# SyncE's queue in a twelve-layer macaron network: the program's order instead of the scheduler's

## The chip, the cores and the metric

The kernel runs on one NeuronCore of a Trainium2 chip. The metric is the device time of one execution in microseconds (us), as the median over runs; lower is better. Times inside the kernel come from one profiled execution.

## What is computed

The input x has 4 x 1024 tokens of 128 features in float32. Twelve residual layers follow each other: three groups of "half a feed-forward, attention, half a feed-forward" whose feed-forwards differ by level, and a fourth of the same shape with ternary weights. Each layer reads a layer norm of x and adds its result to x:

```python
x = x + 0.5 * L0_ffn(norm(x)); x = x + L0_attn(norm(x)); x = x + 0.5 * L0_ffn(norm(x))
x = x + 0.5 * L1_ffn(norm(x)); x = x + L1_attn(norm(x)); x = x + 0.5 * L1_ffn(norm(x))
x = x + 0.5 * L2_ffn(norm(x)); x = x + L2_attn(norm(x)); x = x + 0.5 * L2_ffn(norm(x))
x = x + 0.5 * L3_ffn(norm(x)); x = x + L3_attn(norm(x)); x = x + 0.5 * L3_ffn(norm(x))
```

L0's and L1's attentions are softmax attentions with 16 heads of 8 features (L0's is causal and has more behind it); L2's and L3's are linear attentions. L0_ffn works on values rounded to four-bit floats. What the change bears on most are the mixtures L1_ffn and L2_ffn, where each token goes to two of eight experts. L2's, shortened:

```python
shared = silu(x @ shared_w1.T) @ shared_w2.T
top_k_gates, top_k_idx = top_k(x @ gate_w.T, 2)
gates = zeros((T, 8)); gates[arange(T)[:, None], top_k_idx] = softmax(top_k_gates, axis=1)
h = einsum('td,ehd->teh', x, experts_w1)
expert_out = einsum('teh,edh->ted', silu(h), experts_w2)
out = shared + einsum('ted,te->td', expert_out, gates)
```

L1's expert has two up projections, `silu(g) * u`, and there is no shared part.

## The kernel before

x stays in the on-chip memory SBUF in eight tiles of 512 tokens. The program is written as generators that are advanced in turns: a main line (attention, or one half of a mixture), and beside it side lines such as the routing of the next layer or the return of rows of the last. Behind the written program a scheduler places the instructions: it keeps the data dependencies, and gives each engine (TensorE or PE, VectorE or DVE, ScalarE or ACT, GpSimd or POOL, SyncE or SP) an order of its own planning, which can differ from the order in which the program emits them. An engine then works through its queue strictly in that order; an instruction that waits holds up those behind it.

SyncE computes nothing. It issues nearly all plain transfers and reads registers: the loads of x and of weights (`load` L306, `load_x` L313), the queries and keys of a softmax attention in `laid_out` (L565), the row maxima in `maxima` (L609, L610), everything that a mixture fetches and stores, and the final output (L1232). Gathers and scatters by index are issued by GpSimd.

**A mixture.** There are four mixture layers, numbers 3, 5, 6 and 8 of the twelve layers counted from 0; 3 and 5 are L1's and 6 and 8 L2's. Each is done in two halves of 2048 tokens; "8.1" is the second half of layer 8. The front of a half routes its tokens and scatters their normed rows, sorted by expert, into a buffer `rows_in` in HBM (L1348, GpSimd). The half then runs over 23 tiles of 256 rows, each with one expert's weights. `fetch` gets tile j:

```python
w = pool.tile([P, WIDE], F32, tag="w", name="w", bufs=3)
first = nc.sync.value_load(half.which[:, j : j + 1], min_val=0, max_val=(E - 1) * P)
nc.sync.dma_start(out=w[:, :width], in_=self.weights[bass.ds(first, P), :])
xr = pool.tile([P, RT, D], F32, tag="xr", name="xr", bufs=3)
got = nc.sync.dma_start(out=xr..., in_=k.rows_in[half.h][j * TT : (j + 1) * TT, :]...)
```

That is a register read of the expert's row (L1399), the weights w (L1400; 768 KB in L1, 512 KB in L2) and the rows xr (L1402; 128 KB). w and xr have three buffers each, so a load waits until the tile three before has released its buffer. w is released by the last down matmul (L1447), xr by its transposes (L368, tr<-ident,xr).

`tiles` works on tile j: `turned` transposes the rows on TensorE, and ScalarE copies them to xT (L1420); the up matmuls (L1464) read w and xT; ScalarE and VectorE form h; the down matmuls (L1447) of the tile before follow; `leave` scales the result (yo), transposes it, copies it to yr (L1432, two buffers), and SyncE stores it to `rows_out` (L1433). In the written program, after the first group of up matmuls of tile j:

```python
if c + many == NC:
    ahead = turned(half.fetched[0][1]) if half.fetched else None
yield from downs()
waiting = [(j, w, c + i, h[:, i, :]) for i in range(many)]
if c == 0:
    if j + 2 < NTT:
        self.fetch(half, j + 2)
```

So a fetch is written two tiles ahead of its use, behind the down matmuls of tile j-1, and the transposes of the next tile's rows stand ahead of down matmuls. At the end of a half the first tiles of the next half are fetched, as far as its routing is known. After the last tile, `back` gathers the rows to the tokens (L1515, GpSimd) and VectorE adds them to x (L1502).

**Softmax attention.** Heads are done in groups of four, for a batch of 1024 tokens. For a coming group, `laid_out` brings queries and keys into a buffer `qk` by four transfers (L565); for the running one, `maxima` computes scores (L587), reduces them (L597), and sends the row maxima through memory into a further row of `qk` (L609, L610); the second pass of scores (L747) reads them.

The load of the L3 feed-forward's weights, `l3f_w` (2816 KB), is written where that layer begins, between the halves of layer 8.

Of the kernel before, what the change touches and what calls it, by code (L numbers as in the profile page):

```python
# [1525 lines left out]
def program(arrays):  # L1526
    nc = bacc.Bacc("TRN2", target_bir_lowering=False, num_devices=1)
    ins = {
        k: nc.dram_tensor(f"in_{k}", v.shape, mybir.dt.from_np(v.dtype), kind="ExternalInput").ap()
        for k, v in arrays.items()  # L1530
    }
    out = nc.dram_tensor("out", (B * S, D), F32, kind="ExternalOutput").ap()
    with tile.TileContext(nc) as tc, ExitStack() as ctx:
        _Kernel(ctx, tc, ins, out).run()
    return nc

# [6 lines left out]
```

## Time and profile before

| | |
|---|---|
| median of three runs | 4999.24 us (4991.68 to 5002.0) |
| the profiled execution | 5007.68 us, span 5005.9 us |
| mean granted TensorE clock | 0.909 |
| PE, DVE, ACT, POOL busy | 4282.1, 2664.7, 1707.0, 958.7 us |
| first L0 feed-forward | 0 to 230 us |
| L0 attention | 230 to 1240 us |
| second L0 feed-forward, front of layer 3 | 1240 to 1550 us |
| layer 3 (L1 mixture) | 1550 to 1950 us |
| L1 attention | 1950 to 3100 us |
| layer 5 (L1 mixture) | 3100 to 3450 us |
| layer 6 (L2 mixture), L2 attention begun | 3450 to 3880 us |
| L2 attention, layer 8 (L2 mixture) | 3880 to 4280 us |
| L3 | 4280 to 5006 us |

The profile shows each engine's instructions with start and duration in us. A row of the timeline is: start, duration, engine, line, operation, output<-inputs, shapes, count, and in brackets the idle time just before with what ended it. "SPq" is SyncE's queue: the time that an issue takes there, not that of the transfer. A row of waits is: engine and instruction <- what it waited for: us in total, times, longest. The granted clock is TensorE's, as a share of its full speed. In the timeline four up matmuls of a tile last 1.03 us at the full clock.

### The profile page before, as it was taken

The numbers are of one execution on the slowest core, as the hardware profiler recorded it, in microseconds if no ns is written. First come the engines' busy times: TensorE is split into PE (matmuls) and PEld (weight loads), VectorE is DVE, ScalarE is ACT, GpSimd is POOL, SyncE is SP. The second block draws the span as 40 slices with busy tenths as digits, with TensorE's granted clock in tenths as the row PEclk, the third lists the DMA queues.
The fourth block names the chain that finished last, engine by engine and source line by source line (L and its number), as shares of the span: only waits on it lengthen the run. The fifth ranks groups of instructions, "written<-read, shape, count | busy, mean of one in ns | idle before, by whom it ended". The sixth has DMA issues, their size and how long they took to land.

```text
span 5005.9 us, 62914 instructions
## 1 busy us (share of the span) xinstructions
PE 4282.1 (86%) x23628; PEld 2223.6 (44%) x23628; DVE 2664.7 (53%) x5900; ACT 1707.0 (34%) x3077; POOL 958.7 (19%) x1296
## 2 busy tenths in 40 slices
PE   4799999999757787999999998887877677899999
PEld 3533333333446654333333335765555456344444
DVE  8656757573875353666767673344555544221310
ACT  1134444444222112554545454222222222243322
POOL 4312222221253212001010101213232322200000
PEclk8799999997878897999989999998988798999999
DMA  2000000000002432000010001533332234000000
GB/s 86 5 5 9 3 9 3 9 4 6 1 33 87 152 122 69 6 6 12 8 35 6 12 4 62 170 122 115 113 108 88 74 122 155 20 1 0 0 9 9
DMA packets 112282, 232.51 MB, mean 46 GB/s; under 512 B 20519, under 2 KB 77351, under 8 KB 110315
## 3 DMA queue, kind: packets, MB, share of 16 engines
q1 hardware_dynamic: 95595, 194.91, 12.5%
q0 software_dynamic: 16384, 33.59, 2.3%
q8 instruction: 187, 3.06, 0.3%
q14 instruction: 116, 0.95, 0.1%
HBM read 170.47 MB, written 49.56 MB: 44 GB/s over the span
## 4 chain that ended last, share of the span: by engine, by line
PE 68%; DVE 13%; issue 5%; POOL 5%; another core or an unknown queue 5%; ACT 2%; DMA 1%; SPq 0%; POOLq 0%; DVEq 0%; ACTq 0%
PE sc L747 17%; PE acc L677 9%; PE big L1209 9%; PE big L1464 8%; PE acc L1447 5%; PE big L587 4%; PE tr L368 4%; PE big L1193 1%; POOL ln_rs L355 1%; POOL y L1515 1%; DVE xn L358 1%; PE big L1374 1%; DVE part L597 1%; PE acc L1380 1%
## 5 line engine op out<-in xcount | busy, mean ns | idle before, releaser
L752 ACT ACTIVATE es<-sc 128x512 f32<-128x512 f32 (+3 forms) x1792 | 893.6, 549 | 979.7 <-PE sc L747 566.5
L597 DVE TENSOR_REDUCE part<-big 128x2 f32<-128x1024 f32 (+3 forms) x768 | 886.1, 1158 | 444.7 <-PE big L587 334.6
L747 PE MATMUL sc<-qk 32*128 32x512 f32 (+3 forms) x3584 | 1068.7, 617 | 37.0 <-ACT es L752 29.4
L587 PE MATMUL big<-qk 32*128 32x512 f32 (+3 forms) x3584 | 967.9, 621 | 37.0 <-DVE part L597 17.3
L1464 PE MATMUL big<-xT,w 128*128 128x256 f32 x2208 | 571.9, 398 | 101.3 <-ACT xT L1420 57.3
L747 PEld LDWEIGHTS sc<-qk 32*128 32x128 f32 x3584 | 354.1, 190 | 445.7 <-issue 273.8
L677 PE MATMUL acc<-es,va 128*32 128x256 f32 (+2 forms) x6144 | 528.0, 416 | 1.6 <-POOL es L755 1.4
L1464 PEld LDWEIGHTS big<-xT,w 128*128 128x128 f32 x2208 | 428.9, 200 | 192.6 <-ACT xT L1420 64.4
L1209 PE MATMUL big<-h,l3f_w 128*128 128x512 f32 x1024 | 449.3, 596 | 15.9 <-ACT h L1216 12.6
L355 POOL TENSOR_TENSOR ln_rs<-ln_ve,neg_half 128x4 f32<-128x4 f32 x120 | 124.8, 1041 | 1631.8 <-DVE ln_ve L354 1608.6
L1447 PE MATMUL acc<-h,w 128*128 128x256 f32 x1472 | 393.1, 399 | 37.3 <-DVE h L1361 31.7
L1348 POOL DMA_INDIRECT rows_in<-xn,rows x256 | 249.0, 973 | 571.0 <-DVE rows L1023 163.9
L1515 POOL DMA_INDIRECT y<-rows_out,rows x256 | 244.7, 956 | 542.0 <-DMA xr<-rows_in 242.3
L677 PEld LDWEIGHTS acc<-es,va 128*32 128x32 f32 x6144 | 124.6, 110 | 498.4 <-issue 442.4
L587 PEld LDWEIGHTS big<-qk 32*128 32x128 f32 x3584 | 283.6, 191 | 86.5 <-DVE part L597 38.4
L1447 PEld LDWEIGHTS acc<-h,w 128*128 128x128 f32 x1472 | 279.3, 202 | 86.6 <-DVE h L1361 34.4
L755 POOL TENSOR_SCALAR_AFFINE_SELECT es<-es 128x128 f32<-128x128 f32 x512 | 174.6, 350 | 704.2 <-ACT es L752 698.5
L1209 PEld LDWEIGHTS big<-h,l3f_w 128*128 128x128 f32 x1024 | 192.7, 191 | 252.2 <-issue 231.1
L1472 ACT ACTIVATE h<-big 128x512 f32<-128x512 f32 x184 | 109.7, 597 | 507.7 <-PE big L1464 375.9
L1360 ACT ACTIVATE h<-big 128x1024 f32<-128x1024 f32 x124 | 126.7, 1024 | 431.4 <-PE big L1464 190.9
L1473 DVE TENSOR_TENSOR h<-h,big 128x512 f32<-128x512 f32 x184 | 126.1, 686 | 195.0 <-ACT h L1472 168.9
L358 DVE TENSOR_SCALAR xn<-x,ln_mv,ln_rs 128x128 f32<-128x128 f32 x352 | 108.5, 358 | 194.8 <-POOL ln_rs L355 89.1
(279 smaller groups left out, 4786.6 us busy)
## 6 DMA issues: line engine op xcount, KB each, us to landing
w<-in_l1f_w SPq DMA_DIRECT2D x92, 768.0 KB
w<-in_l2f_w SPq DMA_DIRECT2D x92, 512.0 KB
xr<-rows_in SPq DMA_DIRECT2D x184, 128.0 KB
rows_out<-yr SPq DMA_DIRECT2D x184, 128.0 KB
qk<-qd SPq DMA_DIRECT2D x128, 64.0 KB
rows_in<-zero SPq DMA_DIRECT2D x4, 1472.0 KB
rows_in<-xn,rows POOLq DMA_INDIRECT x256
y<-rows_out,rows POOLq DMA_INDIRECT x256
```

Source lines behind the costliest of these rows:

```text
L355: nc.gpsimd.tensor_tensor(rs, ve, self.neg_half, ALU.pow)
L368: self.nc.tensor.transpose(ps[:n, i * P : (i + 1) * P], t, self.ident)
L587: nc.tensor.matmul(ps[:, j, :w], lhsT=qk[rows, 0, bass.ts(q, P)], rhs=qk[rows, 1, c : c + w], start=True, stop=not diag,)
L597: nc.vector.tensor_reduce(to[:, 2 * pair : 2 * pair + 2, t], ps[:, :, :w], AX.X, ALU.max, negate=True)
L677: nc.tensor.matmul(out[0][32 * i : 32 * i + 32, lo:hi], lhsT=self.vas[b % 2][:, kc, (4 * g + i) * (HD + 1) :][:, :32], rhs=es[i][:, lo:hi] ...
L747: nc.tensor.matmul(ps[:, off:], lhsT=qk[rows, 1, bass.ts(kc, P)], rhs=qk[rows, 0, qb * BLK + off : (qb + 1) * BLK], start=True, stop=True,)
L752: nc.scalar.activation(es[i][:, off:], ps[:, off:], AF.Exp, scale=ISQ)
L1209: nc.tensor.matmul(ps[:, j, :], lhsT=m[:, i * FF + (2 * pair + j) * P : i * FF + (2 * pair + j + 1) * P], rhs=hs[z][:, i, :], start=i == 0 ...
L1348: put = nc.gpsimd.indirect_dma_start(out=k.rows_in[half.h][:, :], out_offset=bass.IndirectOffsetOnAxis(ap=at, axis=0), in_=xns[t // TPB][: ...
L1447: nc.tensor.matmul(outs[j][:, :TT], lhsT=w[:, low + c * D :][:, :D], rhs=h, start=c == 0, stop=c == NC - 1)
L1464: nc.tensor.matmul(ps[:, i, :], lhsT=w[:, bass.ts(col, P)], rhs=xT, start=True, stop=True)
L1515: nc.gpsimd.indirect_dma_start(out=y, out_offset=None, in_=k.rows_out[half.h][:, :], in_offset=bass.IndirectOffsetOnAxis(ap=self.rows[:, i ...
```

## The change

All of SyncE's instructions, transfers and register reads, are put into its queue in the order in which the program emits them. The other engines stay with the scheduler. No transfer is added or removed, and no buffer changes.

```diff
     out = nc.dram_tensor("out", (B * S, D), F32, kind="ExternalOutput").ap()
     with tile.TileContext(nc) as tc, ExitStack() as ctx:
+        ctx.enter_context(tc.manual_schedule(engines={mybir.EngineType.SP}))
         _Kernel(ctx, tc, ins, out).run()
     return nc
```

In SyncE's queue, the steady part of a mixture's half changes as follows (T register read, W weights, x rows, o store of result rows; the number is the tile, here of half 8.1):

```text
before  x14 W12 o9   x15 W13 o10   x16 W14 o11   (T read in batches, far ahead)
after   T12 W12 x12 o9   T13 W13 x13 o10   T14 W14 x14 o11
```

At the beginning of a half, before had W0, W1, W2 ahead, with the rows between them and behind; after has T0 W0 x0, T1 W1 x1, T2 W2 x2. The load of `l3f_w` moves from behind W12 of half 8.0 to the place between the two halves. In the softmax attentions, the four query and key transfers of a coming group stand as a block behind the maxima rows of the group before, where they stood between them.

## The prediction

> **What bounds the kernel now.** I read the page first (engines, then the chain that ended last), then the windows by stage, SyncE's waits, and the timeline of single tiles in the stages where SyncE works.
>
> ```profile
> PE 4282.1 (86%) x23628; PEld 2223.6 (44%) x23628; DVE 2664.7 (53%) x5900; ACT 1707.0 (34%) x3077; POOL 958.7 (19%) x1296
> ...
> PE 68%; DVE 13%; issue 5%; POOL 5%; another core or an unknown queue 5%; ACT 2%; DMA 1%; SPq 0%; POOLq 0%; DVEq 0%; ACTq 0%
> ```
>
> TensorE is busy for 86% of the span and carries 68% of the chain. Data transfers carry 1% and SyncE's queue 0%: today almost nothing waits for what SyncE issues. So little can be won by another order on SyncE, and what it can lose depends on how near its loads stand to their use. That differs by stage:
>
> ```profile
> 1550.00:1950.00 400.00, 334.02 (x1517) 255.12 (x1517) 173.95 (x430) 83.40 (x160) 81.94 (x85) 0.91 0.40 129
> 1950.00:3100.00 1150.00, 1095.03 (x8380) 387.33 (x8381) 733.11 (x1119) 585.22 (x1072) 75.72 (x80) 0.94 0.06 14
> 3450.00:3880.00 430.00, 316.33 (x1360) 230.61 (x1358) 226.32 (x707) 102.72 (x159) 133.80 (x140) 0.87 0.33 102
> 3880.00:4280.00 400.00, 286.36 (x1276) 212.71 (x1276) 205.64 (x588) 97.17 (x154) 118.49 (x123) 0.87 0.35 112
> ```
>
> (Stretch, its length, busy time of PE, PEld, DVE, ACT, POOL, granted clock, DMA share, GB/s.) Attention leaves TensorE 55 us of 1150 and moves 14 GB/s. The mixtures of L1 (first row) and L2 (last two rows) move 102 to 129 GB/s, and there SyncE fetches, tile by tile, the weights (w) and the rows (xr).
>
> ```profile
> 4213.03 1.03 PE L1464 MATMUL big<-xT,w 128*128 128x256 f32 x4
> 4213.23 0.34 SPq L1400 DMA_DIRECT2D w<-in_l2f_w  x1
> 4215.10 0.38 PE L368 MATMUL tr<-ident,xr 128*128 128x128 f32 x2
> 4215.31 1.89 PE L1447 MATMUL acc<-h,w 128*128 128x256 f32 x8
> 4215.51 0.32 SPq L1402 DMA_DIRECT2D xr<-rows_in  x1
> 4217.04 1.03 PE L1464 MATMUL big<-xT,w 128*128 128x256 f32 x4
> 4217.24 0.34 SPq L1400 DMA_DIRECT2D w<-in_l2f_w  x1
> ```
>
> This is the undisturbed tile of L2, 4.01 us from one w load to the next, with TensorE filled. The w issued at 4213.23 went out when the down matmuls of three tiles earlier released its buffer; its up matmuls follow at 4217.04, 3.81 us later. Between them, at 4215.10 (+1.87), TensorE transposes the rows of the very same tile, and only then come the down matmuls that release the next w buffer. The xr issued at 4215.51 isn't this tile's: it takes the buffer that the transposes have just released and serves a tile two further on. Rows are about two tiles ahead of weights in SyncE's queue.
>
> **The change part by part.** Compared by order, TensorE, VectorE, ScalarE and GpSimd keep their steady order; SyncE's alone changes, with the same transfers.
>
> *(1) Rows behind weights.* In program order a fetch issues the register read, then w(j+2), then xr(j+2), and then comes rows_out(j-1). So xr(j+2) leaves right behind w(j+2), which still waits for its buffer. The old trace has this sequence once, by chance, at the start of the last half:
>
> ```profile
> 4128.75 0.34 SPq L1400 DMA_DIRECT2D w<-in_l2f_w  x1
> 4129.14 0.43 SPq L1402 DMA_DIRECT2D xr<-rows_in  x1
> ```
>
> The packets of that xr end at 4132.33, 3.58 us after the w was issued, behind those of the w (4131.99). From last packet to use there is about another half microsecond: where the up matmuls did wait for w, its packets had ended 3.62 after its issue at 4241.28 and the matmul began 4.20 after it,
>
> ```profile
> 4245.48 1.10 PE L1464 MATMUL big<-xT,w 128*128 128x256 f32 x4 [0.23 <-DMA w<-in_l2f_w]
> ```
>
> So the transposes of tile j+2 can start about 3.58 + 0.5 = 4.1 us after w(j+2) was issued, not at +1.87: 2.2 us late. Behind them on TensorE stand the down matmuls (1.9 us) that release the next w, so the delay is inside the loop and comes back in each tile: 4.1 + 0.2 + 1.9 = 6.2 us instead of 4.0. DVE's and ACT's work for the tile, and the row stores, wait for TensorE in the same loop.
>
> Weighed against a rule: the Trainium skill, "DMA: Bandwidth & Descriptors", section "Anatomy of one DMA — SWDGE (gpsimd) path", fits one transfer at 2.0 us plus bytes over 436 GB/s (for GpSimd's path). An estimate from it for 128 KB, issued 0.39 behind w, is 0.39 + 2.3 = 2.7 us, a delay of 0.8 per tile. But it gives 3.2 us for the 512 KB of w, where the trace's use is at 4.2, and it knows no transfer ahead in the queue. I take the row, and keep the rule as a low end.
>
> How many tiles? For each of L2's 92 tiles I took from the timeline the time from the w issue to the transposes of its rows (tr); where that is under 4.1, the tile is late by the difference. Halves are named by the layer's number (0 to 11) and the half, in their order in time:
>
> - 6.0: 13 tiles, 27.4 us; 6.1: 14 tiles, 25.5 us; 8.0: 12 tiles, 22.1 us; 8.1: 20 tiles, 42.2 us. Raw sum 117 us.
>
> The other tiles have attention, routing or shared-expert matmuls between (tr at +4.2 to +13) and don't mind. Part of the sum falls ahead of stalls that have another end: TensorE idles 19.1 us in tile 4 of 6.0, 15.9 and 9.7 in tiles 4 and 5 of 6.1, 11.3 and 13.5 in tiles 2 and 15 of 8.0, 24.1 in tile 4 of 8.1, mostly in VectorE's queue behind gathers of rows (`DVE x L1502 <- DMA y<-rows_out,rows`, 111.1 us in the waits). Those gathers don't move when a tile ahead of them is late. Taking each stall of over 9 us as swallowing what is late before it, there remain 13.0 + 16.2 + 8.6 + 36.7 = 74.5 us; letting every idle of over 2 us swallow, 2.1 + 2.3 + 8.6 + 36.7 = 50 us. I take the middle, **+62 us**. With 3.6 instead of 4.1 (no half microsecond to use) the two are 53.5 and 36; with the rule's 2.7 they are 20 and 17.
>
> *(2) L1's 92 tiles: nothing.* Their tile takes 5.62 us and 768 KB of w; the release of a w buffer stands earlier, and tr comes 7.37 us after w in the undisturbed tile, 5.24 at the least. A w here lands in about 4.0, xr 0.4 to 0.6 behind it, with use at about 5: cover of over 2 us in the steady tile. If that were gone, it would cost up to 1 us for some 45 steady tiles.
>
> *(3) Starts of halves.* Before, three w's were issued ahead, whatever the rows waited for; now w1 and w2 stand behind xr0, which waits for the scatter of its rows. At 8.0 that wait ends at 3912.5; w1 goes out some 0.8 us later and is used at 3918.6 in the old trace, so 0 to +2 us, swallowed by the 11.3 us in tile 2. At 6.0, 6.1 w1 is about 4 us late, ahead of the stalls in tile 4. I put 0 net, bounds 0 and +10.
>
> *(4) The 2816 KB load of l3f_w.* Before, it is issued at 4025.92 in the middle of 8.0 and makes one w land at +7.0 (1.5 us of idle). Now it goes ahead of w0 of 8.1, some 8 us of packets, where tile 4's 24 us hide it. -1.5 to +3; I put 0.
>
> *(5) Register reads.* 23 in each half, 0.57 us each on SyncE. They were hoisted in batches; now one stands ahead of each w, while SyncE waits for the buffer anyway. 0; bare, 0.57 x 30 steady tiles = 17 us.
>
> *(6) Attention.* SyncE's largest waits are here:
>
> ```profile
> SPq L609 <- DVE mrows L607: 1020.4, 58, 55.7
> SPq L565 <- PE sc L747: 386.2, 15, 51.3
> ```
>
> The second is queries of a group two ahead that wait for a buffer, with the maxima rows of the running group behind them. In program order they come after that group's. But TensorE waits for such a transfer (`PE big L587 <- DMA qk<-qd`) only 4.5 us in all. 0, bounds -30 (a third of the 101 us that TensorE idles in both softmax stages) and +10.
>
> **Sum.** 62 + 0. The profiled execution took 5007.68 us (span 5005.9), so it would be 5070; it stands 8.4 above the median of three runs, 4999.24, on which I put the sum: **5061 us**.
>
> **The clock.** Holes of 2.2 us each 6.2 us could throttle TensorE. In the trace a hole of 1.94 us (tile at 1586.8) left the matmuls at 1.03 us for four, but
>
> ```profile
> 3721.85 1.67 PE L1464 MATMUL big<-xT,w 128*128 128x256 f32 x4 [1.96 <-issue]
> ```
>
> shows four matmuls at 1.67 after a hole of 1.96 with another of 1.12 before it. The Trainium skill, "TensorE: Matmul & The Clock Gate", section "HAM oscillation — how this bites in real kernels", tells of a loop with short compute and a wait for each tile that starts cold in every tile, for idle over about 3.4 us. By its limit our hole costs nothing; by the row some windows do. By the row at its worst, 0.6 us per four matmuls, a tile's 16 cost 2.6, times some 28 tiles that keep their delay: +73.
>
> **Rivals.**
>
> *Clock or queue on top (slower still).* The holes throttle, or the delays of (2) and (5) come bare: 62 + 50 gives about 5110, up to 5150. For it: the row above. Against: work stays at two thirds of the time.
>
> *Hidden.* xr lands as the rule says (+17 to +20) and stalls take the rest: 4999 to 5015. For it: half of L2's time already is stalls. Against: the last 18 tiles of 8.1 have none, and their lag is measured from rows.
>
> *Faster.* One mechanism: in attention, loads whose buffer is free no longer stand behind queries whose buffer isn't. Place: L565 ahead of the maxima rows in L1's and L0's attention; price up to -30, with L2's loss at its low 17: -13, 4986. It decides once attention gives back more than L2 loses, so over 50 us by my size, half of TensorE's idle there. Against it: the 4.5 us.
>
> *No effect.* The order would differ on paper only. Against: the order of SyncE's queue in the changed program does differ in each L2 tile.
>
> **How the numbers follow.** A measurement of this kernel can tell about 0.2%, 10 us, from no change. Likeliest case (5035 to 5100): 0.68. Slower still: 0.12. Hidden: 0.10, of which 0.03 ends over +10. Faster: 0.10. So slower 0.83, same 0.07, faster 0.10. Range: from 5000 (half of the hidden case) to 5130.
>
> **What would show it.** In the changed trace: w-to-w in the last half's tiles about 6.2 us; each xr 0.4 behind its w; TensorE's idle ended by xr at the transposes (L368); the stretch of 8.1 longer by some 35 us, L1's mixtures, both softmax attentions and L3 unchanged to within 5; granted clock near 1.0 in the tail. Wrong if the tile stays at 4.0 (xr not late), or if attention moves by over 10 us.

## The result: 2.9% slower, and the profile after

The changed kernel takes 5140.34 us (median of four runs, 5125.11 to 5153.8) against 4996.27: a ratio of 1.0287, 95% interval 1.0254 to 1.0320. The forecast was 5061 us with a range up to 5130. The direction was right, the size was not: +144 us where +62 was worked out. The profiled execution (5135.53 us, span 5133.5) is 128 us above that of before.

The page of the changed kernel, engines and chain:

```profile
PE 4346.9 (85%) x23628; PEld 2252.5 (44%) x23628; DVE 2674.7 (52%) x5900; ACT 1710.7 (33%) x3077; POOL 959.6 (19%) x1296
...
PE 67%; DVE 12%; issue 6%; POOL 6%; DMA 4%; another core or an unknown queue 2%; ACT 2%; SPq 0%; POOLq 0%; DVEq 0%; ACTq 0%
```

Transfers were 1% of the chain and are 4%. Which transfers, the waits of TensorE say for the two L2 mixtures and the linear attention between them (3450 to 4420 us; us in total, times, longest):

```profile
PE tr L368 <- DMA xr<-rows_in: 147.8, 56, 40.3
PE tr L368 <- DVE yo L1426: 38.8, 10, 11.3
PE acc L1447 <- DVE h L1361: 28.4, 4, 19.8
```

The first line is 3% of the span: transposes waiting for rows. In the kernel before, no wait of TensorE is put down to xr. Three of the 56 waits stand at starts of halves. 40.3 us at 8.0 are for the scatter, and TensorE idled there before too (48.9 us, with no releaser named); 8.2 us more are in 8.0 and 13.4 us at the first rows of 8.1. The other 53 add up to 85.8 us. The undisturbed tile, on TensorE and on SyncE (rows of other instructions left out):

```profile
4335.23 1.03 PE L1464 MATMUL big<-xT,w 128*128 128x256 f32 x4
4338.22 0.41 PE L368 MATMUL tr<-ident,xr 128*128 128x128 f32 x2 [1.97 <-DMA xr<-rows_in]
4338.46 1.89 PE L1447 MATMUL acc<-h,w 128*128 128x256 f32 x8
4340.19 1.03 PE L1464 MATMUL big<-xT,w 128*128 128x256 f32 x4
```

```profile
4334.34 0.35 SPq L1400 DMA_DIRECT2D w<-in_l2f_w  x1
4334.74 0.42 SPq L1402 DMA_DIRECT2D xr<-rows_in  x1
4335.88 0.32 SPq L1433 DMA_DIRECT2D rows_out<-yr  x1
4340.39 0.36 SPq L1400 DMA_DIRECT2D w<-in_l2f_w  x1
```

xr goes out 0.40 us behind its w; its transposes begin 3.88 us after the w; the down matmuls follow and release the next w at 4340.39. w to w is 6.05 us instead of 4.01 (the median of the last 17 tiles is 6.01).

By stage, from the first up matmuls of each half in both traces: at the first tile of layer 3 the changed kernel is 13.5 us behind (L0's attention), at layer 6 24.8 (L1's attention), at the last tile of 8.1 125.7. The two L2 mixtures, with the attention between them, thus cost 101 us and the two softmax attentions 29 (13.5 and 15.4); L1's mixtures give back 4, L3 adds 2.

### The profile page after: what moved, and what is told of

Same layout as the page of the kernel before. It is cut to its first block, busy times and chain, and to the rows that moved or that the text cites. A ratio compares the mean times of both kernels' runs of the same rounds, so it can differ in the third digit from the quotient of the medians.

```text
span 5133.5 us, 62740 instructions
## 1 busy us (share of the span) xinstructions
PE 4346.9 (85%) x23628; PEld 2252.5 (44%) x23628; DVE 2674.7 (52%) x5900; ACT 1710.7 (33%) x3077; POOL 959.6 (19%) x1296
## 4 chain that ended last, share of the span: by engine, by line
PE 67%; DVE 12%; issue 6%; POOL 6%; DMA 4%; another core or an unknown queue 2%; ACT 2%; SPq 0%; POOLq 0%; DVEq 0%; ACTq 0%
PE sc L747 17%; PE acc L677 9%; PE big L1209 8%; PE big L1464 6%; PE acc L1447 6%; PE big L587 5%; PE tr L368 4%; DMA xr<-rows_in 3%; POOL y L1515 2%; PE big L1193 1%; POOL rows_in L1348 1%; POOL ln_rs L355 1%; PE big L1374 1%; DVE part L597 1%
## 5 line engine op out<-in xcount | busy, mean ns | idle before, releaser
L1464 PE MATMUL big<-xT,w 128*128 128x256 f32 x2208 | 582.9, 403 | 50.0 <-issue 39.0
L1447 PE MATMUL acc<-h,w 128*128 128x256 f32 x1472 | 406.8, 410 | 32.6 <-DVE h L1361 28.4
```

What stands on the lines that cost most here:

```text
L1447: nc.tensor.matmul(outs[j][:, :TT], lhsT=w[:, low + c * D :][:, :D], rhs=h, start=c == 0, stop=c == NC - 1)
L1464: nc.tensor.matmul(ps[:, i, :], lhsT=w[:, bass.ts(col, P)], rhs=xT, start=True, stop=True)
```

## The experiments

Runs of one group share a chip, and each ratio is to the kernel before beside them. Its level differs from group to group: 4996 us beside the result, 4861 to 4867 in the first two groups and the last, and 5017 in the third. Differences of times are formed within a group. The diffs are shortened to the lines that matter, and their comments are added.

**First group: which part of the program.** The region is opened only for some turns of the main loop in `run`:

```diff
-            for _ in steps:
-                self.tick()
+            if mixture:                      # e_attention: if not mixture
+                with self.tc.manual_schedule(engines={mybir.EngineType.SP}):
+                    for _ in steps:
+                        self.tick()
+            else:
+                for _ in steps:
+                    self.tick()
```

Program order in the mixtures' turns alone:

> SyncE follows the program's order only while a mixture's half is the main line; in the attentions, L0 and L3 the scheduler places its instructions as before. Theory (rows late in L2): xr leaves behind its w as in the changed kernel, an undisturbed tile of L2 takes about 6.0 us instead of 4.0, and some 95 of the 128 us that the profiled executions differ by are here: about 5095 us; both softmax attentions as before. Rival (attention and the clock carry the loss, and L2's stalls absorb the late rows): under 5050. Rival (weights no longer fetched ahead at the starts of halves are what counts): here the scheduler may still place a w across the region's edge, so L2 would lose only some 30 us: about 5030.

4949.95 against 4862.29 us, 1.0176 (1.0159 to 1.0193): +88 us. Half 8.1's tile takes 6.06 us. The larger part of the loss is here, as the theory said. The kernel with the rest:

> The complement: SyncE follows the program's order only while the main line is no mixture (both softmax attentions, the L0 and L3 feed-forwards and linear attentions); in the mixtures the scheduler places it as before. Theory: the tiles of L2 take 4.0 us as before; L1's attention is 15 to 20 us longer, because the scheduler, which plans TensorE with SyncE's order given, groups eight maxima matmuls of a new group together at three of its four batches; with L0's attention +20 to +30 in all: about 5020 us. Rival (the difference in attention is chance of the clock from one execution to the next): 4996 within 10. Rival (attention carries most of the loss): over 5060.

4902.37 us, 1.0079 (1.0062 to 1.0096): +40 us, with the tile at 4.01. Neither rival holds, chance (within 10 us) or most of the loss (over 60 us), and the size is above the 20 to 30 us that were expected.

Then the rows. The changed kernel, with xr written ahead in `tiles`:

```diff
                 if c + many == NC:
                     ahead = turned(half.fetched[0][1]) if half.fetched else None
+                    while half.got < min(NTT, j + 5):
+                        half.ahead.append(self.rows_of(half))     # the xr transfer of fetch, moved here
                 yield from downs()
```

> The changed kernel (SyncE in program order everywhere), but the program itself asks for the rows earlier: xr of tile j+4 is written right behind the transposes that release its buffer, ahead of the down matmuls and of w of tile j+2. Theory: rows are in time, an undisturbed tile of L2 takes 4.0 us again, the 18 tiles at the end of half 8.1 give back 35 us and L2 in all 60 to 90; attention keeps its loss of about 30, the starts of halves 10 to 30: 5040 to 5060 us. Rival (weights' order or register reads slow the tile): the tile stays near 6.0 and the time near 5135.

4886.46 us, 1.0043 (1.0027 to 1.0060): +24 us, about half of what was expected, the tile at 4.01. And the same with program order in the mixtures' turns only:

> Both: SyncE in program order only while a mixture is the main line, and the rows written two tiles further ahead. Theory: the rows are in time and attention is the scheduler's: 4996 to 5020 us, what is left being the starts of halves. Rival: as for the run with program order in the mixtures alone, if rows are not the cause: about 5090.

4850.34 us, 0.9979 (0.9971 to 0.9988): 12 us faster than before. It differs from the first run of this group only in where the program writes xr, and by 100 us. Late rows carry L2's loss, and program order as such costs the mixtures nothing.

**Second group: behind what, and L1's attention.** The kernel before and the changed one, on this chip:

> The kernel before once more, unchanged, for a trace from the same chip as the runs beside it. Both theories: within 0.2% of its own runs, tile of L2 4.0 us.

> The changed kernel once more, unchanged, beside the others on one chip. Theory (a sum of its parts: late rows +100, attention +40): ratio 1.027 to 1.030, tile of L2 5.95 us. Rival (the loss depends on the chip, for instance on its throttling): ratio under 1.02.

Before: 4858.74 us in one run. Changed: 4972.31, 1.0214 (1.0197 to 1.0231), between theory and rival: the tile is 6.03 us, as on the first chip, and from the first tile of layer 6 to the last of 8.1 the traces part by another 96 us, as the 101 there. What is smaller here is the rest. The parts of the first group, 88 and 40, add up to 23 us more than the 105 us of the whole. The traces place most of that in attention: against the one trace of before at this level, L1's attention loses 27 us in the run with program order in the attentions and 9 us in the changed kernel, L0's 26 and 14. For L1 the reason is a wait of 12.7 us that only the whole change removes (shown under "Attention" below).

Next, two statements of `fetch` exchanged:

```diff
-        w = pool.tile(...)
-        first = nc.sync.value_load(...)
-        nc.sync.dma_start(out=w[:, :width], ...)
         xr = pool.tile(...)
         got = nc.sync.dma_start(out=xr..., ...)
+        w = pool.tile(...)
+        first = nc.sync.value_load(...)
+        nc.sync.dma_start(out=w[:, :width], ...)
```

> The changed kernel with two statements of fetch exchanged: the rows xr of tile j+2 are written ahead of the register read and of w of the same tile, so they leave SyncE before it waits for w's buffer, but only one tile earlier than in the changed kernel. Theory (what counts is standing behind a transfer that waits, not how far ahead the program asks): the tile is 4.0 us again, and the ratio that of the run with rows written further ahead, 1.002 to 1.008. Rival (rows must be two tiles ahead): tile over 5 us, ratio over 1.015.

4888.96 us, 1.0043 (1.0026 to 1.0060), the same as with rows written two tiles ahead. Its SyncE:

```profile
4079.78 0.32 SPq L1433 DMA_DIRECT2D rows_out<-yr  x1
4080.14 0.43 SPq L1399 DMA_DIRECT2D xr<-rows_in  x1
4082.57 0.35 SPq L1407 DMA_DIRECT2D w<-in_l2f_w  x1
```

xr leaves 2.43 us before w, while SyncE would otherwise stand waiting for w's buffer. That is enough: w to w settles at 4.01 us in the tiles that follow. So it is not the distance in tiles that counts but standing behind a transfer whose buffer is not free.

L1's attention by itself (the region for that turn only):

> The kernel before with program order on SyncE only while L1's attention is the main line. Compared by order, TensorE's queue then differs from before only at three places, where eight maxima matmuls (L587) stand in a row. Theory: +15 to +25 us, gained at these three places, by TensorE waiting for VectorE's reductions between the matmuls and by the half clock that follows; no wait for a transfer of queries. Rival (late queries or maxima rows in SyncE's queue): TensorE waits on the transfers into qk at the matmuls of L587 or L747. Rival (chance): within 5 us of before.

4891.51 us, 1.0048 (1.0031 to 1.0065): +24.5 us. Against the trace of before, it falls back at about 2020, 2290 and 2575 us by 8, 8 and 9 us, and nowhere else by as much in this stage. The trace counts two instructions for each matmul of the program, so the eight maxima matmuls are 16 in its rows. First the old order at such a place (kernel before, same chip), then the new:

```profile
2018.37 0.70 PE L747 MATMUL sc<-qk 32*128 32x512 f32 x2
2018.38 0.70 PE L587 MATMUL big<-qk 32*128 32x512 f32 x2
2018.90 0.59 PE L747 MATMUL sc<-qk 32*128 32x512 f32 x2
2018.92 0.59 PE L587 MATMUL big<-qk 32*128 32x512 f32 x2
```

```profile
2030.65 1.13 PE L747 MATMUL sc<-qk 32*128 32x512 f32 x4
2031.71 0.64 PE L677 MATMUL acc<-es,va 128*32 128x256 f32 x8
2032.28 1.30 PE L747 MATMUL sc<-qk 32*128 32x512 f32 x4
2034.31 1.79 PE L587 MATMUL big<-qk 32*128 32x512 f32 x8 [0.73 <-DVE qd L558]
2036.77 3.21 PE L587 MATMUL big<-qk 32*128 32x512 f32 x8 [0.67 <-DVE part L597]
```

Score and maxima matmuls use 32 rows of the array each. In pairs they start within 0.02 us of each other, and four and four instructions are done in 1.1 us. Apart, four score instructions take 1.1 to 1.3 us alone, and the maxima come on top; then TensorE waits twice for VectorE, and the second eight run at about half pace, 3.21 instead of 1.79 us (granted clock 0.91 from 2012 to 2042 us, against 1.00 in the kernel before). TensorE's waits in this stage hold no transfer of queries that was not there before.

**Third group: the loop, and controls.** The transposes moved behind the down matmuls, with SyncE's order as in the changed kernel:

```diff
-                if c + many == NC:
-                    ahead = turned(half.fetched[0][1]) if half.fetched else None
                 yield from downs()
+                if c + many == NC:
+                    ahead = turned(half.fetched[0][1]) if half.fetched else None
```

> The changed kernel with one statement of the mixtures' loop moved: the transposes of the next tile's rows (L368, tr<-ident,xr) are written behind the down matmuls instead of ahead of them; SyncE's order is that of the changed kernel, rows right behind their weights. Theory (the late rows are paid in full only because the down matmuls, which release the next w, stand behind the transposes on TensorE): no idle ended by xr is left at the transposes, and a tile of L2 takes about 4.9 us: 4.0 and some 0.9 that the copy xT by ScalarE takes between transposes and up matmuls, now bare; L1's tile grows from 5.6 by as much, so the time alone says little. Rival (the loop doesn't matter, late rows are late in any order): tile of L2 6 us or more, with the idle still ended by xr.

The tile takes 4.68 us (expected 4.9), and the transposes no longer wait:

```profile
4335.86 1.89 PE L1447 MATMUL acc<-h,w 128*128 128x256 f32 x8
4337.59 0.38 PE L368 MATMUL tr<-ident,xr 128*128 128x128 f32 x2
4338.48 1.13 PE L1464 MATMUL big<-xT,w 128*128 128x256 f32 x4 [0.52 <-ACT xT L1420]
```

xr still leaves 0.39 us behind its w. But w is now released ahead of the transposes, so a late row no longer delays the next fetch; what is left is the copy to xT. The time, 5112.37 us, 1.0197 (1.0168 to 1.0225), says little, as expected: L1's tile grows from 5.62 to 5.99 us.

Two controls. The scheduler on SyncE, with the rows written ahead:

> The kernel before (scheduler on SyncE too) with the rows written two tiles further ahead, as in the run that had program order in the mixtures. Compared by order nearly nothing moves. Theory: 1.000 within 0.002, so that the 0.2% of that run comes from program order in the mixtures, once rows are in time. Rival: 0.998, the gain is the earlier rows'.

5022.60 against 5016.58 us, 1.0017 (1.0008 to 1.0026). Earlier rows alone don't give the 0.2% that the last run of the first group gained. And program order in L0's attention alone:

> The kernel before with program order on SyncE only while L0's attention is the main line. Theory: +10 to +20 us (1.002 to 1.004), all in the first hundred microseconds of that stage, by TensorE held at half its clock for longer; no wait for a transfer. Rival (chance of the clock in one trace): 1.000 within 0.0015.

5021.42 us, 1.0012 (1.0003 to 1.0021): +5 us. That is below the theory's 1.002 and within the rival's 0.0015, so the times don't decide. Its trace, the slowest of its 20 executions, falls back by 25 us between 260 and 340 us, with a granted clock of 0.50 from 290 to 310 us where before has 1.00; the medians carry a fifth of it.

**Last: TensorE's order alone.** SyncE's queue as before, instruction by instruction; three times in L1's attention four pairs of maxima matmuls are tied, by an order edge without a wait, behind the second pair of score matmuls after the projections:

```diff
+                            if self.more is not None:      # set when the new batch's values are written
+                                self.more -= 1
+                                if self.more == 0:
+                                    for mm in self.since:  # maxima matmuls since its projections began
+                                        self.tc.add_manual_dep(mm.ins, last.ins.name, BEHIND, reason="in a row")
```

> The kernel before, with SyncE's queue exactly as before (no program order anywhere), but TensorE made to hold back four pairs of maxima matmuls (L587) at the three places in L1's attention where a new batch's projections come in, so that eight of them stand in a row as in the changed kernel. Theory (TensorE's new order is the cause of L1's attention's loss, SyncE's order only the reason for which the scheduler chose it): +15 to +30 us, steps of about 8 us at three places. Rival (SyncE's queue itself causes it): within 5 us of before.

4882.47 against 4861.03 us, 1.0041 (1.0027 to 1.0055): +21 us, with steps of 5, 8 and 5 us at the same three places (at the first of them the clock stays at 1.00), and the same waits between 1930 and 3080 us:

```profile
PE big L594 <- DVE part L606: 16.1, 11, 5.0
PE sc L756 <- DMA qk<-mrows: 12.8, 1, 12.8
```

The first is 10.2 us in the kernel before on the chip of the second group (16.2 in L1's attention alone); the second, 12.7 us, is there too and belongs to SyncE's old order. TensorE's order by itself makes the loss of L1's attention. SyncE's queue is only why the scheduler chose it.

## Why the prediction was wrong in size

**Late rows: right.** The mechanism, the place (L368) and, within 0.2 us, the size per tile are as forecast: xr 0.4 behind w, transposes at +3.9 (forecast 4.1), tile 6.05 (forecast 6.2). The estimate from the Trainium skill's fit for one transfer ("DMA: Bandwidth & Descriptors", "Anatomy of one DMA — SWDGE (gpsimd) path"), 2.7, was set aside for the row, and the measured 3.9 bears that out. The step that says the delay returns in each tile because the down matmuls stand behind the transposes is shown by the moved transposes: 4.68 us. Against the raw sum of 117 us in 59 tiles stand 85.8 us of waits in 53. The last 17 steps of half 8.1 lost 35.3 us (forecast 36.7), and 28.2 us in the traces of the second group.

**The stalls that were to swallow half of it: wrong.** The sum took 117 down to 74.5 and 50, and chose 62, because "those gathers don't move when a tile ahead of them is late". L2 lost 101 us, 96 in the second group: most of the raw sum arrived. Late rows are the cause of nearly all of it: with rows in time the same stretch loses 6 us (two statements exchanged), 1 us (rows ahead, program order everywhere) or nothing (program order in the mixtures only), against 89 us for program order in the mixtures with late rows (all against the second group's trace of before).

Where in the halves it arrives is not firm. In the traces of the first chip the tiles from the sixth to the last lost 15.2, 15.0, 7.4 and 35.3 us, 73 in all, and the first five 8.3, 7.0, 9.8 and 4.8 us, 30 in all, where the prediction had put 0 net; the steps between halves are -1.2, -10.1 and +9.3 us. In those of the second group the two sums are 50 and 51 us. That 73 is the upper of the forecast's two sums is chance.

The stalls did move. At the start of 8.1 the kernel before had the down matmuls of three tiles done when its longest stall began:

```profile
4157.51 2.71 PE L1447 MATMUL acc<-h,w 128*128 128x256 f32 x8
4176.17 2.93 PE L1464 MATMUL big<-xT,w 128*128 128x256 f32 x6 [15.96 <-ACT xT L1420]
```

The changed one stands still with two tiles' up matmuls done and the first tile's down matmuls yet to come:

```profile
4226.50 3.78 PE L1464 MATMUL big<-xT,w 128*128 128x256 f32 x8 [0.52 <-issue]
4250.11 3.78 PE L1447 MATMUL acc<-h,w 128*128 128x256 f32 x8 [19.83 <-DVE h L1361]
```

VectorE's queue had been planned anew: 28 of the 32 additions of gathered rows to x stand ahead of the first tile's h, where before had none, and work of two or three tiles that used to lie ahead of the stall comes after it. But this plan is not what costs the time in 8.1. The runs with rows in time and program order everywhere have 25 and 28 additions there too and lose nothing from the first tile of 8.1 to the last (-1.2 and -0.9 us against before); program order in the mixtures only has none there and loses 36 us in 8.1. How the loss of the first five tiles divides between late rows and stalls was not separated.

**Starts of halves: the term was 0 net, and it was mis-sized.** At 8.0 in the first chip's trace, w1 leaves SyncE 8.4 us behind xr0, where 0.8 was reckoned:

```profile
3972.11 0.70 SPq L1402 DMA_DIRECT2D xr<-rows_in  x1
3980.54 0.70 SPq L1400 DMA_DIRECT2D w<-in_l2f_w  x1
```

Single instructions of the register read between them take 0.70 us there, against 0.02 to 0.35 elsewhere. The second tile loses 14.8 us against before; the third has 8 of these back. The second group's trace has 1.2 us in the same place and no such loss. At 8.1, xr0 stands behind l3f_w: it is used 10.6 us after its issue (3.5 in the steady tile), and the step from the last tile of 8.0 to the first of 8.1 is 9.3 us longer than before, 3.8 in the second group. With rows in time the same wait (13.4 and 13.9 us) is there, and 4 to 5 us of it last to the end of the half.

**Attention: the term was 0, and is 29 us in the traces, 40 in the runs.** The bound of +10 looked only at TensorE's waits for queries (4.5 us, and 4.9 after). It took TensorE's queue as unchanged but for detail, while the changed program has three places with eight maxima matmuls in a row and the one before has none. They cost 21 to 24.5 us when nothing else changes. Attention moved by over 10 us, which the prediction had named as a sign of being wrong.

It also overlooked a gain. In the kernel before, the scheduler put layer 5's first weights and rows into SyncE's queue in the middle of L1's attention. The rows waited there for their scatter (15.9 us), and the maxima rows, which VectorE had written by 2517.3, stood behind them (second group):

```profile
2531.95 1.28 SPq L1402 DMA_DIRECT2D xr<-rows_in  x3
2538.75 0.33 SPq L609 DMA_DIRECT2D mrows<-mrows  x1
2543.43 1.22 PE L747 MATMUL sc<-qk 32*128 32x512 f32 x2 [12.74 <-DMA qk<-mrows]
```

In program order those loads come some 470 us later, and the wait is gone; the trace catches up 14.6 us there. That is the mechanism of the rival "faster", at another place than the one it named and smaller than the loss. So L1's attention loses 15.4 and 9.4 us in the two traces of the changed kernel, and 27 where the old loads stay.

L0's part, 5 us alone or 15 as the difference of 1.0079 and 1.0048, goes with a longer stretch at half the clock: 12 to 31 us between 260 and 340 us in each of the seven traces with program order in L0's attention, none in the others. What starts it, and why the medians show less, was not found.

**The clock.** The forecast put nothing in its sum. Granted in the tail of 8.1 it was 0.93, where the kernel before has 1.00 (first row before, second after):

```profile
4208.00:4254.00 46.00, 45.77 (x229) 37.73 (x228) 23.01 (x35) 14.72 (x24) 0.00 (x0) 1.00 0.57 186
4260.00:4384.00 124.00, 91.41 (x409) 72.80 (x408) 43.56 (x69) 28.63 (x41) 0.00 (x0) 0.93 0.36 122
```

Most tiles there stay at 5.9 to 6.1 us with holes of 1.97, a few take 7 or more; the last sixteen tiles take 101.0 us, 5.8 more than sixteen of 5.95. The rival with throttling in every tile did not come: the clock was halved in four stretches of 3.4 us. The limit in the Trainium skill, "TensorE: Matmul & The Clock Gate", section "HAM oscillation — how this bites in real kernels", idle of over about 3.4 us, would make these holes free; most tiles agree, but 5.8 us of the tail do not.

**Right at nothing:** L1's mixtures (tile 5.62 us before and after) and L3 (2 us in the traces). The register reads and l3f_w were not tried alone. With rows in time L2 loses 1 to 6 us in the traces, so in sum they cost no more than that there.

## What to carry to other kernels

In an in-order queue that issues transfers, put a load whose buffer is already free ahead of one that must wait for its buffer; two exchanged statements were worth 1.7% here. A stall behind a late tile only swallows lateness if its own start doesn't hang on that tile, so keep the full sum in the range. Look in all stages for what an old order holds up, since a change can give something back where nobody looks. And where a scheduler plans the other engines, fixing one engine's order changes the others' too: read each small difference in their queues as a cost of its own.

## What was not expected of the hardware

Matmuls of 32 rows for scores and for maxima ran side by side (starts 0.01 us apart, 0.70 us each), so that taking the pairs apart costs TensorE time with no wait to be seen. And the same kernel before took 4861 to 5017 us from one group of runs to another, 3%, more than the change itself. Its two traces have a mean granted clock of 0.909 (5008 us) and 0.921 (4859 us). The chip alone need not be the reason: the third and the last group carry the same chip number and stand at 5017 and 4861. In the traces of the slower level SyncE takes 0.70 us for one register instruction through stretches of up to 34 us, in those of the faster level only now and then; this was not followed up.
